# Products with C taken for two neighbouring tiles in one GpSimd instruction

## The chip, the core and the metric

The kernel runs on one core of a Trainium2 chip. The metric is device time in microseconds (us) of one execution, lower is better. Engines are called as in the profile: PE (matmul) with PEld (its weight loads), DVE (VectorE), ACT (ScalarE), POOL (GpSimd), SP (the queue that issues the DMAs).

## What is computed

Two layers of a selective state-space block (in-projection, 3x3 depthwise convolution, a scan in four directions, normalization, gate, out-projection) and two layers of attention without softmax and feed-forward in rounded formats, on 4 images of 64 x 64 tokens with 96 channels. Nearly all of the time goes to the scan of the first two layers:

```
def step(h, inp):
    u_t, dt_t, B_t, C_t = inp
    h = jnp.exp(dt_t[..., None] * A) * h + (dt_t * u_t)[..., None] * B_t[:, :, None, :]
    y = jnp.einsum('bkdn,bkn->bkd', h, C_t)
    return (h, y)
```

Here b is the image, k one of 4 directions, d one of 192 inner channels, n one of 16 states, and the scan runs over 4096 positions. For each (b, k, d, n) there is a row of decays exp(delta A), a row of inputs delta u B, the scan of the two, the product with C, and a sum over the 16 states n.

## The kernel before

**Tiles.** Two images are done together, so a layer is two phases, and there are four phases in all. A phase has K = 4 directions times 4 time blocks of TB = 1024 positions: 64 blocks. A block has 48 tiles of 128 x 1024, ordered by image i (2), group g of 32 channels (6) and quarter q of the states (4). The 128 partitions of a tile are 32 channels times 4 states. So there are 3072 tiles; I write tile n of a block as "place" n, 0 to 47, with place = 24 i + 4 g + q.

**One tile n** passes through these steps:

- *decays* (L781, ACT): exp(A delta), 128 x 1024, from `delta`, which `double` (L729) has read from DRAM with each channel repeated over 4 partitions.
- the input delta u B, in one of three ways. Ordinary tiles: PE spreads the B rows into PSUM (`row`, L766) and DVE multiplies them there by `du` (`product`, L788). *Turned* tiles (q = 3 but for g = 0): PE transposes ready products `bt` that ACT made (`fill`, L740). *Pooled* tiles (L37: q = 1, except image 1, group 3, which is place 37): POOL multiplies `du` by the repeated B row `brep` straight into the tile's buffer f (`ahead`, L760); the decays then go to PSUM.
- *scan* (L793, DVE): one scan instruction, from f and the PSUM tile psB into f.
- *remember* (L803, ACT): the last column is copied, as the start of the next block.
- *weigh* (L811, POOL): f is multiplied by the repeated C row `crep`, in place but one column to the left.
- *gather* (L837, PE): 4 matmuls sum over the 4 states of each channel, and over the four q, in a PSUM tile psY; `flush` (L855, ACT) and a DMA take it to `yd` in DRAM, from where `recall` and `resume` add it up over the directions.

**Order.** Every engine's queue is written out by hand in the loop at L1185. Step i of the loop issues work on several tiles: `double` for i+8, `recall` for i+5, `begin` (buffer and decays) for i+2, `ahead` for i+3, `remember` for i-1, `flush` for i-5, `gather` for i-3, `row` for i+2, `scan` of i, the decays of a pooled i+2, `product` of i+1, `weigh` of i. Each engine works its own queue in order and waits for semaphores. So POOL's queue has, in each group of four steps, four `weigh` and one `ahead`, and the `ahead` of tile n stands between the `weigh` of n-4 and of n-3.

**Beside it.** In each step the loop also issues a piece of background work: the convolution of a later phase or the end of an earlier one (L1248), and the preparation of the next block (`prepare`, L565): projections, softplus on ACT, three products `inputs` of 128 x 1024 on POOL (L651, L652), their stores to DRAM, and 48 transposes (`turn`, L663). In a block, `inputs` stand at places 30, 32 and 34, in the first direction of a phase at 34, 36 and 38.

**Buffers.** f has 8 buffers ("flow"), the repeated B and C rows share 8 ("rep"), delta and du together 6 ("dup"), psB and psY have 2 each. After the loop the feed-forward layers reuse these buffers (L1276): 15 tiles for tokens, 13 for transposed tokens.

Of the kernel before, what the change touches and what calls it, by code (L numbers as in the profile page):

```python
# [8 lines left out]
F32 = mybir.dt.float32  # L9
# [6 lines left out]
C = 96  # L16
D = 192
N = 16
# [3 lines left out]
L = HW * HW  # L22
T = 512
NT = L // T
TB = 1024
NTB = L // TB
J = 3
G = 6
Q4 = N // 4
# [5 lines left out]


def pooled(i, g, q):  # L37
    return q == 1 and (i, g) != (1, 3)


def turned(i, g, q):
# [4 lines left out]
def kernel(ctx: ExitStack, tc: tile.TileContext, ins, out, layers=(0, 1, 2, 3)):  # L46
    nc = tc.nc
# [7 lines left out]
    def st(shape, dtype, tag, bufs, name=None):  # L55
        return sp.tile(shape, dtype, tag=tag, name=name or tag, bufs=bufs)

    def psB():
        return ps.tile([128, TB], F32, tag="psB", name="psB", bufs=2)
# [5 lines left out]
        return ps.tile(shape, F32, tag="psM", name="psM", bufs=2)  # L65


    def rep(shape, name):
        return st(shape, F32, "rep", 8, name)

    def flow(shape, name, dtype=F32):
        return st(shape, dtype, "flow", 8, name)

    def part(shape, name):
        return st(shape, F32, "xt", 9, name)
# [2 lines left out]
    def wide(shape, name):  # L78
        return st(shape, F32, "wide", 4, name)
# [155 lines left out]
    def conv_pieces(w, xin, xc, zg, done, moments, settled):  # L235
# [1 line left out]
        norms = []  # L237

        def part_of(n):
            xb = st([C, T], F32, "dup", 6, "xb") if now[0] < 0 else wide([C, T], "xb")  # L240
            nc.sync.dma_start(xb, xin[n // NT][:, n % NT * T : (n % NT + 1) * T])
            return xb

# [3 lines left out]
        for i in range(2):  # L247
# [24 lines left out]
            t = small([C, 1], "grs")  # L272
# [439 lines left out]
    def rows_of(at, i):  # L712

        first = at * per + i * G * Q4
        out = []
        for q in range(Q4):
            for v in (0, 1):
                if v or any(pooled(i, g, q) for g in range(G)):
                    out.append((first + q - (7 if v else 9), at, i, v, q))
        return out  # L720

    def spread(task):

        _, at, i, v, q = task
        r = reps[at, i, v, q] = rep([128, TB], "crep" if v else "brep")
        row = 2 * N * v + N * i + 4 * q
        nc.sync.dma_start(r, made[at]["bc"][row : row + 4].unsqueeze(0).broadcast_to([32, 4, TB]))
# [12 lines left out]
    def fill(task):  # L740
# [4 lines left out]
        for h in range(4):  # L745
            nc.scalar.activation(  # L746
                b.rearrange("p (d h) -> p d h", h=4)[:, :, h], p["dut"][:, i, c, :], AF.Copy, scale=p["turns"][:, c, i, h : h + 1]
            )

    def begin(n):  # L750

        at, i, g, q = tiles[n]
        if pooled(i, g, q):
            scanned[n] = (psB(), early.pop(n))
            return
        f = flow([128, TB + 1], "f")
        scanned[n] = (psB(), f)
        decays(n, f[:, 1:])

    def ahead(n):  # L760

        at, i, g, q = tiles[n]
        f = early[n] = flow([128, TB + 1], "f")
        nc.gpsimd.tensor_mul(f[:, 1:], made[at]["dup"][1, i, g], reps[at, i, 0, q])  # L764

    def row(n):  # L766
        at, i, g, q = tiles[n]
# [35 lines left out]
    def remember(n):  # L803
        at, i, g, q = tiles[n]
        c = (i * G + g) * Q4 + q
        if blocks[at][2] < NTB - 1:
            if at not in states:
                states[at] = st([128, 2 * G * Q4], F32, "state", 2)
            nc.scalar.copy(states[at][:, c : c + 1], scanned[n][1][:, TB : TB + 1])  # L809

    def weigh(n):  # L811
        at, i, g, q = tiles[n]
        f = scanned[n][1]
        nc.gpsimd.tensor_mul(f[:, 0:TB], f[:, 1:], reps[at, i, 1, q])  # L814


    def recall(n):
# [19 lines left out]
    def gather(n):  # L837
        at, i, g, q = tiles[n]
        py = sums[at, i, g]
        f = scanned.pop(n)[1][:, 0:TB]  # L840
        for s in range(4):
            o = 3 - s if made[at]["back"] else s
            multiply(py[32 * o : 32 * o + 32, 0:U4], fold, made[at]["take"](f, s), start=False, stop=(q == Q4 - 1))
# [258 lines left out]

    def flushed(y):

        return L if y is not yd[-1] else max(0, (now[0] - 10) // per - (len(blocks) - NTB)) * TB

    def tail(ph, units=range(L // 256)):
        li, pair = phases[ph]
# [28 lines left out]
    made, reps, sums, states, scanned, early, order = {}, {}, {}, {}, {}, {}, [None]  # L1137
    end = len(tiles)
    now, rest = [-1], (L - TB) // 256
    with tc.manual_schedule(engines=MANUAL):  # L1140
# [41 lines left out]
        rows = sorted(row for at in range(len(blocks)) for i in range(2) for row in rows_of(at, i))  # L1182
        fills = [(at * per + i * per // 2 - 3 + c, at, i, c) for at in range(len(blocks)) for i in range(2) for c in range(NC)]
        waiting = []
        for i in range(-9, end + 6):  # L1185
            while rows and rows[0][0] <= i:
                spread(rows.pop(0))
            if 0 <= i + 8 < end and tiles[i + 8][3] == 0:
                double(i + 8)
            if 0 <= i + 5 < end and tiles[i + 5][3] == 0:  # L1190
                recall(i + 5)
            if 0 <= i + 2 < end:
                begin(i + 2)
            if 0 <= i + 3 < end and pooled(*tiles[i + 3][1:]):
                ahead(i + 3)
            while fills and fills[0][0] <= i:
                fill(fills.pop(0))
            if 0 <= i - 1 < end:
                remember(i - 1)
            if 0 <= i - 5 < end and tiles[i - 5][3] == Q4 - 1:  # L1200
                flush(i - 5)
            if 0 <= i - 3 < end:
                gather(i - 3)
                warm(i - 3)
            if 0 <= i + 2 < end:
                row(i + 2)
            if 0 <= i < end:
                scan(i)
            if 0 <= i + 2 < end and pooled(*tiles[i + 2][1:]):
                decays(i + 2, scanned[i + 2][0])  # L1210
            if 0 <= i + 1 < end:
                product(i + 1)
            if 0 <= i < end:
                weigh(i)
            at, place = divmod(i, per)
            now[0] = i
            if 0 <= i < end:
                if place == 4 and at % (K * NTB) == 0:
                    while aside is not None:
                        advance()  # L1220
                    aside = behind(blocks[at][0])
                plan = at + 1 < len(blocks)
                if plan:
                    if place == 0:
                        made[at + 1], nexts, kept = prepare(*blocks[at + 1])
                        for later, tasks in nexts.items():
                            todo[i + later] = todo.get(i + later, []) + tasks
                    ph1, k1, t1 = blocks[at + 1]
                    if place == min(nexts):
                        need = (t1 + 1) * TB // T if k1 == 0 else NT  # L1230
                        while done[ph1][0] < need:
                            advance()
                    if place == kept[0]:
                        while holds:
                            advance()
                    first = kept[-1] + 4
                    shut = done[0][0] == NT and (kept[0] - 3 <= place < kept[0] or first - 1 <= place < first + 6)
                for what, *arg in todo.pop(i, ()):
                    if what is made[at + 1]["turn"]:
                        waiting.append((what, *arg))  # L1240
                    else:
# [12 lines left out]
        now[0] = end + per  # L1254

        def remaining():
# [18 lines left out]
        spare = flow([128, TB], "spare")  # L1275
# [95 lines left out]
```

## Time and profile before

| what | value |
|---|---|
| time, median of 3 runs | 10528.52 us (10524.45 to 10543.51) |
| profiled execution, its own time | 10533.83 us |
| its span, first to last instruction | 10532.0 us |
| first and last scan start | 166.7 and 9912.1 us |
| POOL, products with C (L814) | 3072 x 2364 ns mean |
| POOL, inputs of pooled tiles (L764) | 704 x 2375 ns mean |
| POOL, `inputs` (L652) | 192 x 2367 ns mean |
| DVE, products with du (L791) | 1728 x 1210 ns mean |
| DVE, scans (L799) | 3072, 2271 to 2344 ns mean by form |
| ACT, copies of the last column (L809) | 2304, median 190 ns |

A duration runs from an instruction's start to its end; the records of two that follow each other overlap a little, so their spacing is what adds up. "Idle before" is the time that an engine stood still ahead of an instruction, and the name after the arrow is what it waited for last.

### The profile page before, as it was taken

How to read it: one execution, taken by the hardware profiler on the slowest of the kernel's cores; microseconds unless marked ns; L12 is line 12 of the kernel's file. 1: busy time of each engine (PE TensorE's matmuls, PEld its weight loads, DVE VectorE, ACT ScalarE, POOL GpSimd, SP SyncE). 2: the span in 40 equal slices, each digit the busy share in tenths (PEclk: the TensorE clock that was granted, in tenths of full speed). 3: DMA queues.
4: the chain of work that ended last, by engine and by line, in shares of the span. 5: the costliest groups of instructions: out<-in, count | busy, mean ns of one | idle time of the engine just before them, and what ended most of it. 6: DMA issues, size and time to landing. Idle time of an engine off the chain costs nothing. (4 is left out here: it accounts for less than half of the span.)

```text
span 10532.0 us, 158718 instructions
## 1 busy us (share of the span) xinstructions
PE 8643.6 (82%) x55291; PEld 4348.5 (41%) x55291; DVE 9423.1 (89%) x5975; ACT 8041.7 (76%) x16147; POOL 9645.1 (92%) x4848
## 2 busy tenths in 40 slices
PE   8998888777888887899878778898888787777777
PEld 2333333333444443333444444333444444334565
DVE  3889999999999999999999999999999999999746
ACT  4777787777788887878787877778777877677676
POOL 3899999999999999999999999999999999999756
PEclk8989898777878888989888888899878887878777
DMA  4568865686568865787555555555555555555310
GB/s 153 184 183 186 187 199 182 176 175 184 183 181 188 187 186 173 195 180 192 186 187 192 181 188 186 182 188 195 189 184 188 190 186 173 172 189 173 117 44 19
DMA packets 1993039, 1837.89 MB, mean 175 GB/s; under 512 B 1391850, under 2 KB 1610092, under 8 KB 1992236
## 3 DMA queue, kind: packets, MB, share of 16 engines
q1 hardware_dynamic: 1992236, 1827.73, 59.0%
q8 instruction: 437, 7.16, 0.3%
q14 instruction: 366, 3.00, 0.1%
HBM read 1439.38 MB, written 387.97 MB: 174 GB/s over the span
## 5 line engine op out<-in xcount | busy, mean ns | idle before, releaser
L814 POOL TENSOR_TENSOR f<-f,crep 128x1024 f32<-128x1024 f32 x3072 | 7186.3, 2364 | 421.9 <-DVE f L799 410.1
L799 DVE TENSOR_TENSOR_SCAN f<-f,state,psB 128x1024 f32<-128x1024 f32 x1776 | 4144.0, 2344 | 344.2 <-PE psB L137 181.2
L784 ACT ACTIVATE f<-delta,L_a 128x1024 f32<-128x1024 f32 x2368 | 2709.7, 1148 | 9.7 <-POOL f L814 1.8
L137 PE MATMUL psB<-spB,sel 96*128 96x512 bf16 x3456 | 1226.5, 442 | 1340.5 <-DVE f L799 1330.3
L791 DVE TENSOR_TENSOR psB<-psB,du 128x1024 f32<-128x1024 f32 x1728 | 2091.3, 1210 | 160.9 <-PE psB L137 156.3
L137 PE MATMUL psY<-f,fold 128*32 128x256 f32 x24576 | 2202.6, 442 | 7.7 <-POOL f L814 7.1
L137 PE MATMUL psB<-ident,bt 128*128 128x128 f32 x10240 | 1764.7, 343 | 215.8 <-DVE f L799 211.7
L137 PEld LDWEIGHTS psB<-ident,bt 128*128 128x128 f32 x10240 | 1627.7, 250 | 608.1 <-DVE f L799 373.3
L746 ACT ACTIVATE bt<-dut,bt 128x192 f32<-128x192 f32 x4096 | 1850.0, 614 | 34.6 <-PE psB L137 32.8
L764 POOL TENSOR_TENSOR f<-du,brep 128x1024 f32<-128x1024 f32 x704 | 1672.1, 2375 | 11.8 <-DMA du<-dud 10.3
L799 DVE TENSOR_TENSOR_SCAN f<-f,psB 128x1024 f32<-128x1024 f32 x592 | 1347.4, 2286 | 135.1 <-PE psB L137 68.3
L799 DVE TENSOR_TENSOR_SCAN f<-psB,state,f 128x1024 f32<-128x1024 f32 x528 | 1229.6, 2329 | 55.4 <-ACT psB L784 55.1
L784 ACT ACTIVATE psB<-delta,L_a 128x1024 f32<-128x1024 f32 x704 | 786.9, 1118 | 644.3 <-DVE f L799 643.2
L137 PEld LDWEIGHTS psY<-f,fold 128*32 128x32 f32 x24576 | 539.0, 115 | 1469.7 <-issue 931.5
L137 PEld LDWEIGHTS <-sel 96*128 96x128 bf16 x3456 | 210.2, 100 | 2216.4 <-DVE f L799 1813.2
L137 PE MATMUL psM<-pad,wf 96*64 96x512 f32 x3132 | 805.8, 624 | 7.5 <-ACT pad L309 5.8
L809 ACT COPY state<-f 128x1 f32<-128x1 f32 x2304 | 437.2, 193 | 268.2 <-DVE f L799 268.0
L671 ACT COPY dut<-psM 128x256 f32<-128x256 f32 x768 | 249.0, 377 | 471.6 <-PE psM L137 471.3
L652 POOL TENSOR_TENSOR xs<-delta,xs 128x1024 f32<-128x1024 f32 x192 | 454.3, 2367 | 63.2 <-ACT delta L649 63.2
L137 PE MATMUL psY<-yold,ident 128*128 128x256 f32 (+1 forms) x1344 | 466.7, 444 | 0.0
L137 PE MATMUL psM<-ident,xs 128*128 128x128 f32 x3072 | 438.0, 289 | 21.0 <-POOL xs L652 18.3
L137 PEld LDWEIGHTS psM<-ident,xs 128*128 128x128 f32 x3072 | 415.1, 202 | 84.0 <-POOL xs L652 28.0
(170 smaller groups left out, 8255.2 us busy)
## 6 DMA issues: line engine op xcount, KB each, us to landing
delta<-deltad SPq DMA_DIRECT2D x768, 512.0 KB
du<-dud SPq DMA_DIRECT2D x768, 512.0 KB
crep<-bc SPq DMA_DIRECT2D x512, 512.0 KB
deltad<-delta SPq DMA_DIRECT2D x192, 512.0 KB
dud<-xs SPq DMA_DIRECT2D x192, 512.0 KB
yd<-ynew SPq DMA_DIRECT2D x768, 128.0 KB
xraw<-xcd SPq DMA_DIRECT2D x144, 512.0 KB
yold<-yd SPq DMA_DIRECT2D x576, 128.0 KB
```

What stands on the lines that cost most here:

```text
L137: nc.tensor.matmul(out, lhsT, rhs, start=start, stop=stop, **kw)
L652: nc.gpsimd.tensor_mul(xs[j], deltas[j], xs[j])
L671: nc.scalar.copy(p["dut"][:, i, h * NC // 2 : (h + 1) * NC // 2, 64 * j : 64 * j + 64], m[:, :, 64 * i : 64 * i + 64])
L746: nc.scalar.activation(b.rearrange("p (d h) -> p d h", h=4)[:, :, h], p["dut"][:, i, c, :], AF.Copy, scale=p["turns"][:, c, i, h : h + 1])
L764: nc.gpsimd.tensor_mul(f[:, 1:], made[at]["dup"][1, i, g], reps[at, i, 0, q])
L784: nc.scalar.activation(out, made[at]["dup"][0, i, g], AF.Exp, scale=W[phases[ph][0]]["a"][:, k, g, q : q + 1])
L791: nc.vector.tensor_mul(scanned[n][0], scanned[n][0], made[at]["dup"][1, i, g])
L799: nc.vector.tensor_tensor_scan(f[:, 1:], a, bu, 0.0 if t == 0 else states[at - 1][:, c : c + 1], ALU.mult, ALU.add)
L809: nc.scalar.copy(states[at][:, c : c + 1], scanned[n][1][:, TB : TB + 1])
L814: nc.gpsimd.tensor_mul(f[:, 0:TB], f[:, 1:], reps[at, i, 1, q])
```

## The change

Two tiles 2p and 2p+1 (q = 0, 1 or q = 2, 3) now share one buffer f of 128 x 2 x 1025, and the C rows come in pairs too. `weigh` is issued at odd steps only, for both tiles: 1536 instructions on 128 x 2 x 1024 instead of 3072 on 128 x 1024. `remember` copies two columns at even steps. All q = 1 tiles are pooled, place 37 with them: 64 more `ahead` on POOL, 64 fewer `product` on DVE and 64 fewer pairs of `row` matmuls on PE. `gather` moves from i-3 to i-5, `flush` from i-5 to i-7, `resume` from i-2 to i-4. `double` moves from i+8 to i+6, with 4 buffers for delta and du instead of 6, `recall` from i+5 to i+3. f has 5 buffers of two tiles instead of 8 of one, C rows 3 buffers of two rows, the B row 2 buffers of its own. The tail has 13 tiles for tokens instead of 15, and 16 for transposed tokens.

```
 def pooled(i, g, q):
-    return q == 1 and (i, g) != (1, 3)
+    return q == 1
...
+    def flow():
+        return st([128, 2, TB + 1], F32, "flow", 5, "f")
...
     def rows_of(at, i):
         first = at * per + i * G * Q4
-        ...
-                    out.append((first + q - (7 if v else 9), at, i, v, q))
+        return [(first - 8, at, i, 0), (first - 6, at, i, 1), (first - 1, at, i, 2)]
     def spread(task):
...
+        _, at, i, v = task
+        row = 2 * N * (v > 0) + N * i + (4, 0, 8)[v]
+        if v == 0:
+            r = reps[at, i, "b"] = st([128, TB], F32, "brep", 2)
+            parts = [r]
+        else:
+            r = reps[at, i, v - 1] = st([128, 2, TB], F32, "crep", 3)
+            parts = [r[:, 0], r[:, 1]]
+        for m, to in enumerate(parts):
+            rows = made[at]["bc"][row + 4 * m : row + 4 * m + 4]
+            nc.sync.dma_start(to, rows.unsqueeze(0).broadcast_to([32, 4, TB]))
...
-            r = p["dup"][v, i, g] = st([128, TB], F32, "dup", 6, ("delta", "du")[v])
+            r = p["dup"][v, i, g] = st([128, TB], F32, "dup", 4, ("delta", "du")[v])
...
+    def place_of(n):
+        if n // 2 not in two:
+            two[n // 2] = flow()
+        return two[n // 2][:, n % 2]
     def begin(n):
+        scanned[n] = (psB(), place_of(n))
+        if not pooled(*tiles[n][1:]):
+            decays(n, scanned[n][1][:, 1:])
...
     def ahead(n):
         at, i, g, q = tiles[n]
-        f = early[n] = flow([128, TB + 1], "f")
-        nc.gpsimd.tensor_mul(f[:, 1:], made[at]["dup"][1, i, g], reps[at, i, 0, q])
+        nc.gpsimd.tensor_mul(place_of(n)[:, 1:], made[at]["dup"][1, i, g], reps[at, i, "b"])
...
-            nc.scalar.copy(states[at][:, c : c + 1], scanned[n][1][:, TB : TB + 1])
+            nc.scalar.copy(states[at][:, c : c + 2], two[n // 2][:, :, TB])
     def weigh(n):
         at, i, g, q = tiles[n]
-        f = scanned[n][1]
-        nc.gpsimd.tensor_mul(f[:, 0:TB], f[:, 1:], reps[at, i, 1, q])
+        f = two[n // 2]
+        nc.gpsimd.tensor_mul(f[:, :, 0:TB], f[:, :, 1:], reps[at, i, q // 2])
...
-        for i in range(-9, end + 6):
+        for i in range(-9, end + 8):
...
-            if 0 <= i + 8 < end and tiles[i + 8][3] == 0:
-                double(i + 8)
-            if 0 <= i + 5 < end and tiles[i + 5][3] == 0:
-                recall(i + 5)
+            if 0 <= i + 6 < end and tiles[i + 6][3] == 0:
+                double(i + 6)
+            if 0 <= i + 3 < end and tiles[i + 3][3] == 0:
+                recall(i + 3)
...
-            if 0 <= i - 1 < end:
-                remember(i - 1)
-            if 0 <= i - 5 < end and tiles[i - 5][3] == Q4 - 1:
-                flush(i - 5)
-            if 0 <= i - 3 < end:
-                gather(i - 3)
-                warm(i - 3)
+            if 0 <= i - 2 < end and i % 2 == 0:
+                remember(i - 2)
+            if 0 <= i - 7 < end and tiles[i - 7][3] == Q4 - 1:
+                flush(i - 7)
+            if 0 <= i - 5 < end:
+                gather(i - 5)
+                warm(i - 5)
...
-            if 0 <= i < end:
+            if 0 <= i < end and i % 2:
                 weigh(i)
...
-            if 0 <= i - 2 < end and tiles[i - 2][3] == 0:
-                resume(i - 2)
+            if 0 <= i - 4 < end and tiles[i - 4][3] == 0:
+                resume(i - 4)
...
-            "xt": several(6, [128, Q, C], F32, "dup", 6, "xt") + several(9, [128, Q, C], F32, "xt", 9, "xt"),
-            "tT": several(8, [C + 1, TB], F32, "rep", 8, "tT") + several(5, [C + 1, TB], F32, "flow", 8, "tT"),
+            "xt": several(4, [128, Q, C], F32, "dup", 4, "xt") + several(9, [128, Q, C], F32, "xt", 9, "xt"),
+            "tT": several(2, [C + 1, TB], F32, "brep", 2, "tT") + halves,
```

POOL's new queue in steps 4k-3 to 4k is: the pair (4k-4, 4k-3), `ahead` of tile 4k+1, the pair (4k-2, 4k-1). On PE, `gather` of tile n stands behind `row` of n+6 instead of n+4.

More of the change, by code (lines that the diff above doesn't have):

```diff
@@ L65, in psM @@
         return ps.tile(shape, F32, tag="psM", name="psM", bufs=2)
[L68 to L72, printed above, removed]
+    def flow():
+        return st([128, 2, TB + 1], F32, "flow", 5, "f")
     def part(shape, name):
@@ L239, in part_of @@
         def part_of(n):
-            xb = st([C, T], F32, "dup", 6, "xb") if now[0] < 0 else wide([C, T], "xb")
+            xb = st([C, T], F32, "dup", 4, "xb") if now[0] < 0 else wide([C, T], "xb")
             nc.sync.dma_start(xb, xin[n // NT][:, n % NT * T : (n % NT + 1) * T])
@@ L714, in rows_of @@
         first = at * per + i * G * Q4
[L715 to L718, printed above, removed]
-                    out.append((first + q - (7 if v else 9), at, i, v, q))
-        return out
-    def spread(task):
[L724 to L727, printed above, removed]
+        return [(first - 8, at, i, 0), (first - 6, at, i, 1), (first - 1, at, i, 2)]
+    def spread(task):
+        _, at, i, v = task
[9 more added lines that the diff above has]
+            nc.sync.dma_start(to, rows.unsqueeze(0).broadcast_to([32, 4, TB]))
     def double(n):
@@ L748, in fill @@
             )
+    def place_of(n):
+        if n // 2 not in two:
+            two[n // 2] = flow()
+        return two[n // 2][:, n % 2]
     def begin(n):
[L752 to L758, printed above, removed]
+        scanned[n] = (psB(), place_of(n))
+        if not pooled(*tiles[n][1:]):
+            decays(n, scanned[n][1][:, 1:])
     def ahead(n):
         at, i, g, q = tiles[n]
-        f = early[n] = flow([128, TB + 1], "f")
-        nc.gpsimd.tensor_mul(f[:, 1:], made[at]["dup"][1, i, g], reps[at, i, 0, q])
+        nc.gpsimd.tensor_mul(place_of(n)[:, 1:], made[at]["dup"][1, i, g], reps[at, i, "b"])
     def row(n):
@@ L840, in gather @@
         f = scanned.pop(n)[1][:, 0:TB]
+        if n % 2:
+            two.pop(n // 2)
         for s in range(4):
@@ L1103, in flushed @@
     def flushed(y):
-        return L if y is not yd[-1] else max(0, (now[0] - 10) // per - (len(blocks) - NTB)) * TB
+        return L if y is not yd[-1] else max(0, (now[0] - 12) // per - (len(blocks) - NTB)) * TB
     def tail(ph, units=range(L // 256)):
@@ L1136 @@
     per = 2 * G * Q4
-    made, reps, sums, states, scanned, early, order = {}, {}, {}, {}, {}, {}, [None]
+    made, reps, sums, states, scanned, two, order = {}, {}, {}, {}, {}, {}, [None]
     end = len(tiles)
@@ L1273, in several @@
             return [st(shape, dtype, tag, bufs, name) for _ in range(n)]
-        spare = flow([128, TB], "spare")
+        halves = [h for n, tag in ((3, "crep"), (4, "flow")) for t in several(n, [128, 2, TB], F32, tag, n + (n == 4), tag)
+                  for h in (t[0 : C + 1, 0], t[0 : C + 1, 1])]
+        spare = flow().rearrange("p m t -> p (m t)")
         pools = {
-            "xt": several(6, [128, Q, C], F32, "dup", 6, "xt") + several(9, [128, Q, C], F32, "xt", 9, "xt"),
-            "tT": several(8, [C + 1, TB], F32, "rep", 8, "tT") + several(5, [C + 1, TB], F32, "flow", 8, "tT"),
+            "xt": several(4, [128, Q, C], F32, "dup", 4, "xt") + several(9, [128, Q, C], F32, "xt", 9, "xt"),
+            "tT": several(2, [C + 1, TB], F32, "brep", 2, "tT") + halves,
             "tn": several(3, [128, Q, C + 1], F32, "delta", 3, "tn"),
```

## Prediction

> **What bounds the kernel now.** First the page's busy times, to see which engines can be the bound:
>
> ```profile
> PE 8643.6 (82%) x55291; PEld 4348.5 (41%) x55291; DVE 9423.1 (89%) x5975; ACT 8041.7 (76%) x16147; POOL 9645.1 (92%) x4848
> ```
>
> POOL and DVE are both near full. These shares hold a slow start (three blocks of about 170 us while the first convolutions run) and a tail of 620 us, so I read the table of stretches for the 61 blocks between:
>
> ```profile
> core 0: us, PE busy (x) PEld busy (x) DVE busy (x) ACT busy (x) POOL busy (x), PEclk, DMA share, GB/s
> 676.00:9912.00 9236.00, 7595.13 (x48668) 3728.91 (x48670) 8665.14 (x4804) 7184.68 (x14265) 8848.42 (x3893) 0.84 0.63 184
> ```
>
> There POOL is busy 95.8% and DVE 93.8%. Which one holds the other is told by the waits of the same stretch (total us, times, longest):
>
> ```profile
> PEld psY L137 <- POOL f L814: 332.2, 418, 1.6
> POOL f L814 <- DVE f L799: 324.2, 314, 4.2
> ...
> DVE f L799 <- PE psB L137: 238.7, 223, 5.7
> ```
>
> POOL's `weigh` waits for DVE's scan; DVE's scan waits for PE, never to speak of for POOL. So DVE with its PE stalls sets the pace, and POOL follows 0.1 to 5 us behind. But POOL has only 4% in hand, so I look at where in a block it is short. This is block 54, POOL alone, from place 28 on:
>
> ```profile
> 8481.58 4.66 POOL L814 TENSOR_TENSOR f<-f,crep 128x1024 f32<-128x1024 f32 x2 [1.22 <-DVE f L799]
> 8486.20 2.37 POOL L764 TENSOR_TENSOR f<-du,brep 128x1024 f32<-128x1024 f32 x1
> 8488.54 2.36 POOL L814 TENSOR_TENSOR f<-f,crep 128x1024 f32<-128x1024 f32 x1
> 8490.85 2.38 POOL L652 TENSOR_TENSOR xs<-delta,xs 128x1024 f32<-128x1024 f32 x1
> 8493.19 4.65 POOL L814 TENSOR_TENSOR f<-f,crep 128x1024 f32<-128x1024 f32 x2
> 8497.78 2.39 POOL L652 TENSOR_TENSOR xs<-delta,xs 128x1024 f32<-128x1024 f32 x1
> 8500.10 4.72 POOL L814 TENSOR_TENSOR f<-f,crep 128x1024 f32<-128x1024 f32 x2
> 8504.77 2.37 POOL L652 TENSOR_TENSOR xs<-delta,xs 128x1024 f32<-128x1024 f32 x1
> 8507.10 6.97 POOL L814 TENSOR_TENSOR f<-f,crep 128x1024 f32<-128x1024 f32 x3
> 8514.02 2.39 POOL L764 TENSOR_TENSOR f<-du,brep 128x1024 f32<-128x1024 f32 x1
> ```
>
> and DVE at its end:
>
> ```profile
> 8507.59 1.21 DVE L791 TENSOR_TENSOR psB<-psB,du 128x1024 f32<-128x1024 f32 x1
> ...
> 8520.56 2.33 DVE L799 TENSOR_TENSOR_SCAN f<-psB,state,f 128x1024 f32<-128x1024 f32 x1
> ```
>
> From 8481.58 on POOL never rests: the three `inputs` (L652) fall here, and place 37, in this very stretch, has no `ahead`. The L764 at 8514.02 makes the input of place 41 and ends at 8516.41; the scan that needs it starts at 8520.56. That slack, 4.15 us here, is on average 3.77 us over the 64 blocks (half of them 3.2 to 4.2, the least 1.1).
>
> **The change, part by part.**
>
> *Pairs on POOL.* In that timeline three `weigh` take from 8507.10 to 8514.02, four elsewhere 9.27 us: the spacing is 2.316 us, that of L764 2.33. What a pair saves is the part of an instruction that doesn't grow with its columns. Small instructions show it:
>
> ```profile
> 9994.08 0.21 POOL L925 TENSOR_TENSOR spare<-spare 128x8 f32<-128x8 f32 x1
> 9994.24 0.21 POOL L926 TENSOR_TENSOR spare<-spare 128x8 f32<-128x8 f32 x1
> ```
>
> 0.165 us apart for 8 columns. Then a column costs (2.316 - 0.165)/1016 = 2.117 ns, the fixed part is 0.148 us, and a pair takes 4.484 us. No instruction of two long rows is in the trace. The cheap bound is 4.40 (all of a small one's 0.21 us saved, and a little), the dear one 4.632 (two instructions' worth; a line through the 384 columns of L1045, 0.875 us apart, leaves next to no fixed part). I take 4.48, since L925 is the nearest in types: POOL does 1536 x 0.148 = 227 us less.
>
> *Place 37 pooled.* POOL gets 64 x 2.33 = 149 us, DVE loses 64 products of 1.21 us and their gap, 1.25 each in the spacing: **-80 us** on the engine that sets the pace. PE loses 64 pairs of `row` matmuls, behind other work: 0. Decays into psB can stall DVE: 81.1 us for 704 such tiles in the whole span, so **+7** for 64 more.
>
> *What is late next.* DVE's next wait is for POOL at place 41. Lay the new queue of block 54 against its recorded scans. Scan 29 ends at 8483.74. The pair (28, 29) can start only then, whereas the product of 28 was done before. From there to the end of `ahead`(41): 5 pairs, 3 `ahead` (33, 37, 41), 3 `inputs` of 2.34: 5 x 4.484 + 3 x 2.33 + 3 x 2.34 = 36.4 us, hence 8520.3 instead of 8516.4, 3.9 later. Scan 41 could start 1.25 earlier, at 8519.3. So DVE stalls 1.0 us there and keeps 0.25 of the 1.25. In general the stall is 3.9 + 1.25 - slack, with the mean slack 1.4 us per block. The same lay-out of POOL's queue over all 64 blocks, with the recorded ends of scans and DVE's stalls passed on, gives 81 us, 69 of them at place 41 and 12 at 45 (59 with pairs of 4.40, 102 of 4.55, 128 of 4.632). The same bookkeeping of the old queue gives POOL's recorded lag at every place to within 0.7 us. I take **+81**.
>
> The product with du takes 1210 ns on DVE (L791) and the one that replaces it 2375 on POOL (L764). The Trainium skill speaks against such a move: its page "GPSIMD Engine Reference", section "4.1 Engine selection", sends two-input elementwise work to VectorE, since GpSimd takes about twice as long; the two rows agree on the ratio. By that rule place 37 would have stayed on DVE, with neither the 80 us nor the 81, and the sum below would hardly differ.
>
> *Sums five behind.* A tile's sum needs both of its pair's products. Before, PE's `gather`(n) stood ahead of `row`(n+5), which needs scan n+3: with three steps of 9236/(61 x 48) = 3.15 us, 2.3 us for `weigh` and 0.6 for the matmuls, a lag of 6.6 us of POOL was free. Now the sum of a pair's first tile m stands ahead of `row`(m+7), which needs scan m+5, four steps after scan m+1: 12.6 - 4.5 - 0.6 = 7.5 us are free. In DVE's waits for psB, 69 us (66 cases) are ones where PE itself had waited for POOL after the PSUM tile was free. Between all of it kept and all gone I take half, **-35**; lags in the first half of a block get smaller by the lay-out, those at place 39 larger (5.1 us mean).
>
> *Pairs on ACT.* 1152 fewer copies of 190 ns, 219 us of ACT, which is busy 78% there. DVE waits 74 us for ACT in the main stretch: 0 to -20, I take **-5**.
>
> *Four delta and input buffers.* SP now waits in `double`(n) for product n-6 (before: n-10). From the end of that product to the first use, recorded: `ahead`(n+1) 12.9 us or more, decays (n) 7.6 or more, median 11.6. Laying the packets' bytes in the order of issues, these DMAs land 2.9 (delta) and 3.5 us (du) after issue, at most 7.9. Behind a waiting `double` on SP stand stores of `flush` and loads of `recall`, both with several steps in hand. Cost 0 to +10, taken 0. The second pair of C rows waits for the product of place 21 or 45 and has 11 us or more until its use; POOL already holds SP there 715 us without anyone waiting. Taken 0.
>
> *Later `inputs`.* Their third ends up to 2 us later, and `turn` on PE waits for it (28 us now): **+5** (0 to 20).
>
> *The end.* The last pair ends 2.2 us later, and two tiles fewer in the tail hold back two loads: **+5** (-10 to +20).
>
> Sum: -80 + 7 + 81 - 35 - 5 + 5 + 5 = **-22 us**. Against the profiled execution's 10533.83 us that is 10512; it lies 5.3 us above the median of the runs shown, so against the median I expect **10506 us**. A measurement of this kernel tells about 0.2% (21 us) from no change, so this is just on that bound.
>
> **The rivals.**
>
> *The stall at place 41 doesn't come* (15%). PE and ACT work on while DVE stalls, and the PE stalls after place 41 (30 us at place 43, 19 at 47, more in the next block's first places) could absorb it. For it: those stalls exist. Against: most of them are `row` work that starts only when a scan frees psB, so they move along with it. Then -80 + 7 - 35 - 5 + 5 + 5 = -103, **10425**; half absorbed, 10465.
>
> *The pair costs as much as two, so that the change doesn't do what it says and POOL becomes the bound in places 30 to 45* (33%). POOL then gets 149 us more and nothing back; the stall is 128 us, no PE wait goes: -80 + 7 + 128 + 5 + 5 - 5 = +60, **10588**, slower. It decides from about 4.55 us per pair on (102 us of stall, net zero). For it: the 384-column line. Against: the small rows.
>
> *A late delta* (7%). If one group in four gets its delta 1 us late, 192 us, 10700. Against: the leads above.
>
> *My forecast* (45%), 10480 to 10540.
>
> **The numbers.** Faster by over 0.2% (below 10507): half of my forecast's cases (0.24) and the first rival (0.15), 0.39. Within 0.2%: the rest of the forecast but its dear end (0.18) and the cheap end of the second rival (0.02), 0.20. Slower (above 10550): what is left of the second rival (0.31), the third (0.07) and the forecast's dear end (0.03), 0.41. The range goes from half-way into the first rival to the second's price: 10445 to 10590.
>
> **What would show it.** The group L814 with 128x2x1024: 1536 of some 4530 ns (duration; 4660 or more speaks for the second rival). A new row in the waits, DVE f <- POOL f L764, of 60 to 100 us, with place 41 in nearly all of it. DVE's L791 down by 64. PEld psY <- POOL well below 332 us. No row of ACT or POOL waiting for the DMAs of delta and du. I am wrong if DVE does not wait for POOL's L764 at all, or if it waits for POOL at places away from the `inputs`.

## The result and the profile after

The changed kernel takes **10670.28 us** (median of 4 runs, 10665.92 to 10674.65) against 10529.51 us before in the same runs: ratio 1.0132, 95% interval 1.0114 to 1.0149, 141 us slower. The forecast was 10506; the range ended at 10590. The profiled execution took 10665.92 us with a span of 10663.9.

The page's busy times of the changed kernel:

```profile
PE 8674.7 (81%) x55152; PEld 4351.0 (41%) x55152; DVE 9355.3 (88%) x5911; ACT 7949.7 (75%) x14995; POOL 9040.3 (85%) x3376
```

POOL has 605 us less to do than before and DVE 68 us less, and the kernel is slower. So neither is what was lost; a wait must have grown. The groups show the parts of the change at work (columns: count | busy us, mean ns of one | idle before it, its releaser):

```profile
L814 POOL TENSOR_TENSOR f<-f,crep 128x2048 f32<-128x2048 f32 x1536 | 6416.4, 4182 | 1142.1 <-DVE f L799 1103.2
...
L764 POOL TENSOR_TENSOR f<-du,brep 128x1024 f32<-128x1024 f32 x768 | 1813.5, 2361 | 23.3 <-DMA du<-dud 20.2
```

A pair lasts 4182 ns, and where nothing holds POOL up its next instruction starts 4.135 us after the pair (median of some 980 cases); I had taken 4.484, with 4.40 as the cheap bound. POOL is cheaper than forecast, and L764, the row that place 41 waits for, hardly holds up DVE. This is the whole span's wait of DVE for it, forecast at 60 to 100 us (us, times, longest):

```profile
DVE f L799 <- POOL f L764: 8.5, 12, 1.6
```

The waits between 676 and 10050 us, which cover the same blocks as before's 676 to 9912:

```profile
POOL f L814 <- DVE f L799: 985.6, 701, 4.9
...
DVE f L799 <- PE psB L134: 427.3, 279, 5.5
...
PEld psY L134 <- POOL f L814: 106.0, 160, 3.5
...
ACT f L784 <- DMA delta<-deltad: 63.2, 18, 8.4
```

POOL now waits for DVE three times as long as before (324.2), and PE waits for POOL a third as long (332.2), the latter as forecast. But **DVE waits for PE's psB 427 us instead of 239**. That wait I had expected to shrink.

To see which tiles it hits, I averaged for every place the time from the end of the scan before to the end of its own, over blocks 4 to 61, in both traces. Place 37 goes from 3.57 to 2.28 us, the product that left. Place 41 rises by 0.08. The intervals of the *turned* tiles (q = 3) rise: place 23 goes from 2.34 to 3.65, and 7, 11, 15, 31, 35, 39 and 47 rise by 0.17 to 0.34 each, all ten together by 3.4 us. A block takes 153.5 instead of 151.3 us. The first scan starts at 162.4 us and the last at 10038.9: the stretch between is 131 us longer, and the tail behind it 5 us.

Block 54 at place 23, before (start, us; the background work between left out):

```profile
8456.81 2.33 DVE L799 TENSOR_TENSOR_SCAN f<-psB,state,f 128x1024 f32<-128x1024 f32 x1
...
8458.77 0.64 PE L137 MATMUL psY<-f,fold 128*32 128x256 f32 x8
8459.05 1.21 DVE L791 TENSOR_TENSOR psB<-psB,du 128x1024 f32<-128x1024 f32 x1
...
8459.34 2.05 PE L137 MATMUL psB<-ident,bt 128*128 128x128 f32 x16
...
8460.36 4.59 DVE L799 TENSOR_TENSOR_SCAN f<-f,state,psB 128x1024 f32<-128x1024 f32 x2
```

Scan 21 frees its PSUM tile at 8459.1. `row`(23), the 16 transposes into it, starts 0.2 us later and ends at 8461.4, long before scan 22 does; scans 22 and 23 follow without a gap (one line, x2). The same place after:

```profile
8555.69 2.33 DVE L799 TENSOR_TENSOR_SCAN f<-psB,state,f 128x1024 f32<-128x1024 f32 x1
...
8557.93 1.21 DVE L791 TENSOR_TENSOR psB<-psB,du 128x1024 f32<-128x1024 f32 x1
...
8558.24 1.22 PE L134 MATMUL psY<-yold,ident 128*128 128x128 f32 x4
...
8559.24 2.35 DVE L799 TENSOR_TENSOR_SCAN f<-f,state,psB 128x1024 f32<-128x1024 f32 x1
...
8559.39 1.08 PE L134 MATMUL psY<-f,fold 128*32 128x256 f32 x8
8560.40 3.63 PE L134 MATMUL psB<-ident,bt 128*128 128x128 f32 x16
...
8564.15 2.35 DVE L799 TENSOR_TENSOR_SCAN f<-f,state,psB 128x1024 f32<-128x1024 f32 x1 [2.55 <-PE psB L134]
```

Scan 21 ends at 8558.0. PE now takes `resume` (psY<-yold) first, then `gather`, and only at 8560.40, 2.4 us after the tile was free, the transposes. They also last 3.63 us instead of 2.05. The granted clock (PEclk, the third column from the end) is 0.55 there and was 1.00 in the stretch of before, and 2.05/0.55 is 3.7:

```profile
8459.30:8461.40 2.10, 2.10 (x21) 1.94 (x18) 2.00 (x2) 2.04 (x6) 2.10 (x2) 1.00 0.35 127
...
8560.40:8564.10 3.70, 3.70 (x21) 3.58 (x18) 1.19 (x1) 2.16 (x8) 3.70 (x2) 0.55 0.58 171
```

DVE stands still for 2.55 us.

**The theory** from here on: `resume`(4k) stood at the end of step 4k+2, so that the next `row` on PE's queue was that of tile 4k+5, which is pooled and has none. Moved from i-2 to i-4 it stands at the end of step 4k+4, right ahead of `gather`(4k) and `row`(4k+7), a turned tile's 16 transposes, for which DVE has hardly any slack. **Rivals:** the pairs come too late for their sums; the four delta and input buffers; the later `flush`; the pooled place 37.

### The profile page after: what moved, and what is told of

Read it like the earlier page. It is cut to its first block, busy times and chain, and to the rows that moved or that the text cites. A ratio compares the mean times of both kernels' runs of the same rounds, so it can differ in the third digit from the quotient of the medians.

```text
span 10663.9 us, 154483 instructions
## 1 busy us (share of the span) xinstructions
PE 8674.7 (81%) x55152; PEld 4351.0 (41%) x55152; DVE 9355.3 (88%) x5911; ACT 7949.7 (75%) x14995; POOL 9040.3 (85%) x3376
## 5 line engine op out<-in xcount | busy, mean ns | idle before, releaser
L814 POOL TENSOR_TENSOR f<-f,crep 128x2048 f32<-128x2048 f32 x1536 | 6416.4, 4182 | 1142.1 <-DVE f L799 1103.2
L799 DVE TENSOR_TENSOR_SCAN f<-f,state,psB 128x1024 f32<-128x1024 f32 x1728 | 4035.2, 2345 | 482.3 <-PE psB L134 323.7
L784 ACT ACTIVATE f<-delta,L_a 128x1024 f32<-128x1024 f32 x2304 | 2613.3, 1144 | 106.1 <-DMA delta<-deltad 63.2
L791 DVE TENSOR_TENSOR psB<-psB,du 128x1024 f32<-128x1024 f32 x1664 | 2012.7, 1210 | 161.3 <-PE psB L134 152.0
L764 POOL TENSOR_TENSOR f<-du,brep 128x1024 f32<-128x1024 f32 x768 | 1813.5, 2361 | 23.3 <-DMA du<-dud 20.2
L134 PE MATMUL psB<-ident,bt 128*128 128x128 f32 x10240 | 1691.8, 332 | 15.6 <-DVE f L799 14.7
L784 ACT ACTIVATE psB<-delta,L_a 128x1024 f32<-128x1024 f32 x768 | 860.3, 1120 | 866.0 <-DVE f L799 861.9
L799 DVE TENSOR_TENSOR_SCAN f<-psB,state,f 128x1024 f32<-128x1024 f32 x576 | 1340.9, 2328 | 57.2 <-ACT psB L784 50.0
L134 PE MATMUL psY<-yold,ident 128*128 128x256 f32 (+1 forms) x1344 | 559.0, 523 | 0.0
L799 DVE TENSOR_TENSOR_SCAN f<-psB,f 128x1024 f32<-128x1024 f32 x192 | 435.7, 2269 | 26.2 <-ACT psB L784 24.4
```

The source lines that it names most:

```text
L134: nc.tensor.matmul(out, lhsT, rhs, start=start, stop=stop, **kw)
L764: nc.gpsimd.tensor_mul(place_of(n)[:, 1:], made[at]["dup"][1, i, g], reps[at, i, "b"])
L784: nc.scalar.activation(out, made[at]["dup"][0, i, g], AF.Exp, scale=W[phases[ph][0]]["a"][:, k, g, q : q + 1])
L791: nc.vector.tensor_mul(scanned[n][0], scanned[n][0], made[at]["dup"][1, i, g])
L799: nc.vector.tensor_tensor_scan(f[:, 1:], a, bu, 0.0 if t == 0 else states[at - 1][:, c : c + 1], ALU.mult, ALU.add)
L814: nc.gpsimd.tensor_mul(f[:, :, 0:TB], f[:, :, 1:], reps[at, i, q // 2])
```

## The experiments

Ratios are to the kernel before in the same runs, with 95% intervals. Differences in us are between medians; the kernel before itself came out at 10529.5 to 10534.8 in the five sets of runs, and the intervals reach 10 to 19 us to each side, so a difference between two runs is good to some 20 us. The waits shown are those between 676 and 10050 us. The number in a name such as "five behind" is `gather`'s distance.

**1. `resume` alone put back**, in the changed kernel.

```
-            if 0 <= i - 4 < end and tiles[i - 4][3] == 0:
-                resume(i - 4)
+            if 0 <= i - 2 < end and tiles[i - 2][3] == 0:
+                resume(i - 2)
```

> The changed kernel with one thing undone: `resume` is issued for tile i-2 again instead of i-4; `gather` stays five behind. Theory (order on PE): in the changed kernel `resume` (0.7 to 1.2 us of PE) falls into the step ahead of the turned tile's `row` (16 transposes, 2 to 3.6 us), where before it fell into the step ahead of a pooled tile, which has no `row`. Of the 3.4 us per block that scans of turned tiles gained, 2 to 2.5 go: 10520 to 10550 us; the wait of place 23 falls from 1.35 us to below 0.5. Rival A (four delta and input buffers, later transfers): 10670, unchanged. Rival B (sums wait for the coarser pairs): unchanged, 10670.

10598.77 us, 1.0063 (1.0048 to 1.0078): half of the loss goes, less than I expected. Place 23 is back at 2.35 us. A new wait takes the rest, for the PSUM tile that a `flush` seven steps behind frees too late:

```profile
PEld psY L134 <- ACT ynew L863: 563.6, 361, 6.2
...
PE psY L134 <- ACT ynew L863: 364.8, 255, 5.7
```

It hits places 18 and 19 (4.08 and 2.57 us instead of 3.57 and 2.35). So this run can't price `resume` by itself.

**2. All sums three behind**, as in the kernel before (`gather(i - 3)`, `flush(i - 5)`, `resume(i - 2)`), with the pairs.

> The changed kernel with the sums three behind as before: `gather` i-3, `flush` i-5, `resume` i-2; pairs, place 37, four buffers stay. Theory (order on PE): all 3.4 us per block of added waits at turned tiles go and the 80 us of place 37 stay: 10460 to 10500 us. Rival A (four buffers): 10670. Rival B (the pair's products come too late for the sums, so that five behind is needed): PE waits for POOL's L814 rise above 500 us and the time stays above 10600.

10748.69 us, 1.0204 (1.0189 to 1.0219): my expectation was wrong and the rival's right. Place 23 is back (2.39), but now PE waits for POOL's pairs, and DVE behind it at places 39 (5.21 us instead of 2.67) and 43 (3.44):

```profile
PEld psY L134 <- POOL f L814: 557.3, 422, 4.5
...
PE psY L134 <- POOL f L814: 341.4, 256, 4.3
```

**3. Sums four behind** (`gather(i - 4)`), with `flush` at i-6 and `resume` at i-3, in the changed kernel.

> The changed kernel with the sums four behind: `gather` i-4, `flush` i-6, `resume` i-3. Theory (order on PE): `resume` now falls into the step ahead of an ordinary `row` (0.6 us), so the 1.3 us of place 23 and most of the rest at turned tiles go; POOL's pairs leave a little less room than five behind, so places 39 and 43 (after POOL's `inputs`) may keep some of it: 10480 to 10540 us. If the sums themselves must be five behind for the pairs, 10600 or more, with place 39 as in the run with three behind.

10517.00 us, 0.9984 (0.9975 to 0.9993), as the theory said: 153 us under the changed kernel, with place 23 at 2.54.

**4. The order of the sums without the pairs**: the kernel before with `gather` at i-5, `flush` at i-7, `resume` at i-4, `double` at i+6, `recall` at i+3, four delta and input buffers, 9 buffers for f, and place 37 left on DVE.

> The kernel before, single tiles and place 37 on DVE, with the later sums (`gather` i-5, `flush` i-7, `resume` i-4, `recall` i+3), four delta and input buffers with `double` i+6, and 9 buffers f. Theory (order on PE): turned tiles wait as in the changed kernel, about 200 us more than before: 10690 to 10750 us. Rival B (pairs): 10530, as before. Rival A (four buffers) agrees with the theory here, and is told apart by the runs with the sums moved back.

10718.87 us, 1.0174 (1.0157 to 1.0191): the whole loss and more, without any pair and with place 37 on DVE. Place 23 is at 3.50. This clears the pairs and the pooled place 37.

**5. Only the four buffers**, in the kernel before (`double` at i+6).

> The kernel before with four delta and input buffers and `double` at i+6, nothing else. Theory: the leads of 7.6 us or more against landings of 7.9 at most cost nothing, 10525 to 10545 us, so that the 184 us of the kernel before with the later sums are those of the sums. Rival A: a good part of the 184 us, 10580 or more, with ACT waiting for the DMA of delta.

10563.54 us, 1.0023 (1.0013 to 1.0033): some 24 us (14 to 35) by the ratio, where I expected 10525 to 10545 us. Two waits are new:

```profile
POOL f L764 <- DMA du<-dud: 20.0, 11, 5.8
ACT f L784 <- DMA delta<-deltad: 19.7, 10, 4.7
```

They are few. Ahead of ACT's three longest (blocks 4 and 28) SP stands 4.6 to 6.1 us at a store of `flush` (L862), with `double` queued behind it. I had priced this at nothing. But the waits for the DMAs need not be what costs the 24 us: in this trace DVE's waits grow most at places 23 and 24, for PE (13.7 and 7.9 us), where none of the longer DMA waits falls. The way to the loss stays open.

**6. Only place 37 pooled**, in the kernel before, with single products.

> The kernel before with place 37 pooled and nothing else. The lay-out of the prediction for single tiles: `ahead` of place 41 ends 2.33 us later and its scan could start 1.25 earlier, against a mean slack of 3.77 us: DVE waits some 0.4 us per block there, so -80 + 7 + 25 = 10480 us. If POOL (92% busy) is the bound instead, 149 us of added POOL work shows: 10530 to 10600.

10591.41 us, 1.0055 (1.0040 to 1.0070), slower, where I expected faster. Place 37 falls to 2.28 as it should, but 39 rises by 1.19 us and 43 by 0.55:

```profile
PEld psM L137 <- POOL xs L652: 108.4, 47, 4.8
...
PE psM L137 <- POOL xs L652: 86.0, 44, 4.3
```

POOL's lateness doesn't reach DVE by way of L764; it goes through PE, which waits in `turn` for the third of the `inputs` with the next tile's `row` queued behind.

**7. The changed kernel with place 37 on DVE.**

```
-    return q == 1
+    return q == 1 and (i, g) != (1, 3)
```

> The changed kernel with place 37 back on DVE. With pairs of 4.14 us POOL has room, so place 37 should be worth its 80 us of DVE: 10740 to 10755 us. If it costs more than it gives, as it did with single tiles (57 us), 10600 to 10620.

10725.12 us, 1.0177 (1.0162 to 1.0192): 55 us slower than the changed kernel, a little less than the 70 to 85 that I expected. Pooling place 37 loses 57 us with single products (run 6) and gains 55 with pairs. The rule of the Trainium skill's page "GPSIMD Engine Reference", section "4.1 Engine selection", which the prediction weighed, says VectorE; here it would have cost those 55 us. That fits POOL's time in hand: it waits 986 us for DVE in the changed kernel.

**8. Five behind, with `flush` and `resume` a step earlier**, in the changed kernel.

```
-                flush(i - 7)
+                flush(i - 6)
...
-                resume(i - 4)
+                resume(i - 3)
```

> The changed kernel with `gather` five behind, but `resume` at i-3 and `flush` at i-6: `resume` falls ahead of an ordinary `row`, and the PSUM tile that it takes was flushed two steps earlier, as before. Theory (order on PE): 10460 to 10500 us, with neither the wait of place 23 nor PE's waits for ACT's `flush` that the run with `resume` at i-2 showed (928 us). If the place of `resume` is not the cause, 10600 to 10670.

**10498.57 us, 0.9963 (0.9948 to 0.9978)**: two lines, 172 us less than the changed kernel, faster than both. In the window (which here takes in 176 us of the tail) DVE's wait for psB is back where it was before the change:

```profile
DVE f L799 <- PE psB L134: 239.6, 238, 6.0
```

**9. `flush` alone a step earlier**, in the changed kernel.

> The changed kernel with `flush` one step earlier (i-6 instead of i-7) and nothing else. It is the other half of the best version, which moved `flush` and `resume` together. Theory (only the place of `resume` on PE's queue costs the time): 10650 to 10680 us, as the changed kernel, with the interval up to scan 23 still near 3.6 us. Rival (the late `flush` on ACT was what cost it): 10500 to 10550 us, place 23 near 2.4 us.

10679.03 us, 1.0143 (1.0126 to 1.0160), as the changed kernel; place 23 at 3.72. DVE's wait:

```profile
DVE f L799 <- PE psB L134: 398.4, 266, 6.1
```

Runs 8 and 9 differ in `resume` alone, by one step, so it is `resume`'s step that brings run 8's gain. That the `flush` has to come along is argued from run 1; `resume` at i-3 with `flush` at i-7 was not run.

**10. The order of run 8 without the pairs**: run 4 with `flush` at i-6 and `resume` at i-3.

> The kernel before, single products, place 37 on DVE, with the four delta and input buffers and sums five behind as in the changed one (9 buffers for f), but `flush` at i-6 and `resume` at i-3, so that `resume` doesn't stand ahead of a turned tile's `row`. Theory (sums five behind cost nothing by themselves, `resume`'s place cost some 150 us, the four buffers some 30): 10530 to 10580 us, against 10719 with `resume` at i-4; place 23 back to about 2.4 us. Rival (the later sums cost time with single products wherever `resume` stands): 10650 us or more.

10544.03 us, 1.0013 (1.0003 to 1.0023): 175 us less than run 4. With `resume` in this place, five behind costs nothing that shows beside run 5's buffers. What pairs and place 37 are worth together is the step from here to run 8: 1.0013 to 0.9963, 53 us.

The runs side by side. "Late" is the mean time from the end of scan 21 to the start of `row`(23) on PE, from the traces:

| kernel | `resume` | late, us | up to scan 23, us | block, us | time, us |
|---|---|---|---|---|---|
| before | i-2 | 0.43 | 2.34 | 151.3 | 10529.5 |
| changed | i-4 | 1.82 | 3.65 | 153.5 | 10670.3 |
| run 9 | i-4 | 1.93 | 3.72 | 153.6 | 10679.0 |
| run 4, single products | i-4 | 1.75 | 3.50 | 154.3 | 10718.9 |
| run 7, place 37 on DVE | i-4 | 1.86 | 3.72 | 154.5 | 10725.1 |
| run 8 | i-3 | 0.50 | 2.44 | 150.7 | 10498.6 |
| run 10, single products | i-3 | 0.40 | 2.34 | 151.3 | 10544.0 |

Whatever else differs, the four kernels with `resume` at i-4 are late and the others are not (runs 1 to 3 have 0.52, 0.44 and 0.60 us). It is so at all ten places of turned tiles: their `row` starts 0.67 us after its PSUM tile is free in the kernel before (mean of the ten places, blocks 4 to 61), 1.32 us in the changed one and 0.70 in run 8.

At place 23 the row is also slower: the 16 transposes last over 3 us in 5 of 58 blocks before, in 30 after and in 6 in run 8. Over all ten places, though, such slow rows become fewer, 246 of 580 before and 184 after, so a lower clock is not what all of them have in common. How much of place 23's 1.31 us is lateness and how much the clock was not told apart. Why the granted clock moves with the order was not tried.

**11. What a product of two rows costs on POOL, alone.** The first of three kernels of POOL products only.

> This kernel leaves all of the reference's computation out and writes zeros: it only issues products of two tensors on POOL, 8 of each form back to back: contiguous rows of 8 to 4096 columns, and the in-place product shifted by one column on 1x1024, 2x1024 and 2x512 columns, alone and beside scans on DVE. Theory (a column's price falls with the length of the instruction, and what was mis-sized in the prediction is the straight line through the short rows): 1x1024 spaced 2.29 to 2.33 us and 2x1024 4.10 to 4.17 us alone and beside scans alike, and the plain rows of 1024 and 2048 columns the same as the in-place ones, so the saving of about 0.5 us per pair belongs to the length, not to the shape. Rival (POOL is faster in the changed kernel only because something else on the chip leaves it more room): 2x1024 alone 4.45 to 4.63 us, twice the single one less a fixed part of 0.15 us or less.

Plain products of 2048 columns, the pair of the changed kernel, one such row of 1024, and two rows of 512 in one instruction (mean ns of 8):

```profile
L39 POOL TENSOR_TENSOR o<-a,b 128x2048 f32<-128x2048 f32 x8 | 35.7, 4493 | 0.0
...
L52 POOL TENSOR_TENSOR f<-f,c 128x2048 f32<-128x2048 f32 x8 | 33.2, 4156 | 0.0
...
L47 POOL TENSOR_TENSOR f<-f,c 128x1024 f32<-128x1024 f32 x8 | 18.5, 2337 | 14.6 <-DVE f L33 14.4
...
L57 POOL TENSOR_TENSOR f<-f,c 128x1024 f32<-128x1024 f32 x8 | 17.2, 2172 | 0.0
```

The straight line of the prediction was right for plain rows. The pair is cheaper, not for its length (two times 512 are cheaper than 1024 as well). Both theories named the length or the surroundings; both fall.

**12. Which part of the form saves**: two rows with a gap in some operands, in place or not, shifted by 1 or 8.

> This kernel leaves all of the reference's computation out and writes zeros: POOL products alone, 8 of each form: two rows of 1024 with a gap between rows in all, in some or in none of the operands, in place and not, two of 512, four of 256, 512 and 1024, one of 1024. Earlier, alone on the chip, the in-place 2x1024 took 4156 ns and the plain 2048 took 4493. Theory (rows with a gap in the operand that is written or read make a column cheaper, 1.94 instead of 2.10 ns): in-place 2x1024 4156 ns with gaps of 1 and of 16 columns alike, 4x512 the same, 4x1024 some 8130 against 8802 for 4096 plain ones, and rows without a gap, which the instruction can join into one, 4493. Rival 1 (the saving is a part per row, not per column): 4x256 is cheaper than the 2172 of 2x512 by as much as 2x512 is than 2338, 0.17 us. Rival 2 (being in place is what saves): 2x1024 with gaps that isn't in place takes 4493.

Of these forms, only those in place, shifted by one, with rows 1025 columns apart are cheap: 2x1024 4164 ns, 4x512 4223, 2x512 2219, 4x256 2229, 4x1024 8190. The same two rows not in place take 4518, and rows 1040 apart with a shift of 8 take 4508. The theory falls, and rival 1 with it. Rival 2's figure for rows not in place came about, but being in place is not enough: the rows 1040 apart and a single row (2402 ns) are in place too, and dear.

**13. On which column a row starts.**

> This kernel leaves all of the reference's computation out and writes zeros: POOL products alone, 8 of each form. Earlier forms told that only the in-place product shifted by one column whose rows start 1025 columns apart is cheap (4.16 instead of 4.50 us for 2x1024; 4.51 with rows 1040 apart and a shift of 8, and whenever it isn't in place). Theory (the second row is the cheap one, since it starts at an odd column: out on an odd column, in on the next even one): the second row of 1024 alone takes about 2.00 us, the first 2.34; rows 1040 apart that start on column 1 with a shift of 1 take 3.82 for two, those that start on column 0 4.50. Rival (what saves is the two rows in one instruction, wherever they start): each row alone takes 2.34 and two rows 1040 apart with a shift of 1 take 4.16 from column 0 and 1 alike.

First row and second row of a pair alone, then two rows 1040 apart, both begun on column 0 (L45) or on column 1 (L47):

```profile
L45 POOL TENSOR_TENSOR h<-h,c 128x2048 f32<-128x2048 f32 x8 | 35.6, 4483 | 0.0
...
L47 POOL TENSOR_TENSOR h<-h,c 128x2048 f32<-128x2048 f32 x8 | 30.2, 3807 | 0.0
...
L31 POOL TENSOR_TENSOR f<-f,c 128x1024 f32<-128x1024 f32 x8 | 18.4, 2336 | 6.9 <-DVE f L28 6.9
...
L33 POOL TENSOR_TENSOR f<-f,c 128x1024 f32<-128x1024 f32 x8 | 15.7, 1994 | 0.0
```

As the theory said: the saving is not in the pairing. The second row is cheap because of the column that it starts on. A row that writes from column 1, reads from column 2 and takes the other factor from column 0 costs 1.99 us; from 0, 1 and 0 it costs 2.34. Not in place it is 1.99 as well. A row written from column 1 and read from column 8 (2333 ns), or one whose other factor starts on column 1 (2336), is dear. Starting columns of the three operands that all differ modulo 4 fit every form of runs 11 to 13; why, no run tells.

**14. All rows of the cheap kind, in run 8's order.**

```
-        return st([128, 2, TB + 1], F32, "flow", 5, "f")
+        return st([128, 2, TB + 4], F32, "flow", 5, "f")[:, :, 1 : TB + 2]
```

> The best version so far (pairs, five behind, `flush` at i-6, `resume` at i-3) with each row of f begun one column later and rows 1028 instead of 1025 columns apart, so that both rows of a pair are of the cheap kind, not only the second. The pair should take 3.82 us instead of 4.17, POOL some 540 us less in all. Theory (POOL has time in hand in this version and DVE with its PE stalls is the bound): 10470 to 10500 us, little under 10499. Rival (the lag of POOL behind the scans still costs, by way of `gather` on PE: PE waits 145 us for it): 10400 to 10450 us.

**10471.91 us, 0.9940 (0.9923 to 0.9957)**, the fastest of all. A pair lasts 3815 ns, POOL has 550 us less to do, and the time falls by 27 us (the two intervals still overlap a little).

**15. The same in the kernel before**, single products.

> The kernel before, single products, with each f begun one column later (4 spare columns), so that every product with C is of the cheap kind: 2.00 instead of 2.34 us, 3072 x 0.34 = 1040 us of POOL in all, without any other change of the order. It asks what POOL's time was worth in the kernel before. Theory (DVE with its PE stalls sets the pace, POOL only follows; only the 69 us of DVE's waits behind PE waits for POOL can go): 10450 to 10520 us. Rival (POOL at 96% was a bound of its own): 10300 to 10400 us.

10527.38 us, 0.9993 (0.9984 to 1.0003), which is less gain than even the theory's 10450 to 10520 us. The page and the group:

```profile
PE 8687.3 (82%) x55291; PEld 4363.7 (41%) x55291; DVE 9411.9 (89%) x5975; ACT 8044.4 (76%) x16147; POOL 8585.9 (82%) x4848
...
L814 POOL TENSOR_TENSOR f<-f,crep 128x1024 f32<-128x1024 f32 x3072 | 6128.6, 2003 | 1456.1 <-DVE f L799 1418.3
```

POOL loses 1059 us of its 9645 and the kernel does not move. POOL, with the highest share of all engines, was worth nothing by itself here. Where POOL's time did pay was run 7, in which a product could be moved onto it (place 37).

## Why the prediction was wrong, step by step

**The step that failed is *Sums five behind*, "I take half, -35".** I counted how much of POOL's lag a later `gather` makes free. PE's wait for POOL did fall, from 332 to 106 us, but that is not this step's alone: with single products and a better place for `resume` (run 10) it falls from 353 to 310 us over the whole span. And the step moves `resume` too, and I didn't ask what stands behind it on PE's queue in its new place. It is the `row` of a turned tile. In place of -35 the order cost 172 us (changed kernel less run 8; 155 in single products, run 4 less run 5). With `resume` a step earlier the same five behind shows -11 us by the ratios and -20 by the medians, with an uncertainty of 15 (run 10 less run 5): at most a part of the gain of 35, and no loss from five behind as such. None of my rivals held it: all were about POOL or a DMA, none about the order on PE.

*Stall at place 41, +81:* 8.5 us in all. This was a size: 4.484 us for the pair, where it took 4.135, below my cheap bound of 4.40 too. Five pairs stand ahead of `ahead`(41), so that the error is 1.7 us per block, more than the mean slack that I found missing (1.4). The fixed part of 0.148 us was right for plain rows (run 11); half of the rows were of a cheaper kind, which none of the rows that I had read shows. Run 8, where DVE waits for PE no longer than before the change, keeps it at 11 us, so it isn't the new stalls that hide it.

*Place 37, -80:* place 37's interval falls by 1.29 us, 83 us in 64 blocks, as forecast; taking it back in the changed kernel costs 55 (run 7), good to some 20. With single products (run 6) the same edit loses, by a path that I had priced at +5 (`turn` waits for the `inputs`). *Later `inputs`, +5:* in the changed kernel PE waits 43 us for them, as before (25.5 and 17.1 us before, 26.3 and 16.4 after), nothing. *Decays into psB, +7:* DVE's wait for them went from 81.1 to 74.8 us, nothing. *Pairs on ACT, -5:* the copies take 217 us less, as counted, but ACT as a whole only 92; what of it reaches the end wasn't told apart. *Four delta and input buffers, 0:* 24 us (run 5), by a path that stays open. *The end, +5:* 617.6 to 622.6 us, as forecast, but this can't be told from scatter: runs 6 and 15, whose tail is that of before, have 613.7 and 622.4.

With the runs' values the sum is -83 + 0 + 9 + 172 + 24 + 5 = 127 us, against 141 measured. With run 7's 55 in place of 83 it is 155. Both are within what the single terms are uncertain by (some 20 us each).

Of my signs, the L764 wait (8.5 instead of 60 to 100) and the DMA waits (63 us for delta) told at once that DVE's loss lay elsewhere than forecast. The 128x2048 group at 4182 instead of 4530 ns spoke against my price and against the second rival alike.

## What to carry to other kernels

When a step of a queue written by hand is moved, write down for each instruction that moves what is queued behind it in the new place and how much slack that has. Here about a microsecond of PE work ahead of a turned tile's transposes cost up to 1.3 us a block at one place; a step earlier, ahead of an ordinary `row`, it cost nothing that shows. An engine's high share alone does not tell its worth: here 1059 us off the busiest engine gave nothing, and a move of two lines in the changed kernel gave 172. Price a new form of an instruction by itself before its count is multiplied by thousands.

## What the runs showed of the hardware

- A POOL product of 128 x 1024 in 32-bit takes 1.99 or 2.34 us depending only on the columns on which its operands start (run 13), and four spare columns took 15% off the products with C in the kernel before (2364 to 2003 ns, run 15).
- Beside scans whose two operands both lie in SBUF, POOL's products and DVE's scans take turns in run 11: single products follow each other every 4.28 us and pairs every 6.10, one scan to each, where a scan alone takes 2.18. In the kernel the scan reads one operand from PSUM, and neither is stretched in this way (4.135 us for a pair there, 4.11 alone; 2.27 to 2.35 us for a scan). The Trainium skill's page "SBUF — State Buffer", section "Who interferes with whom", says that a DVE instruction with two SBUF inputs contends with a GpSimd instruction that reads SBUF, and that one with at most one, outside the 2-port modes, does not; both cases agree.
- The same 16 transposes took 2.05 us at a granted clock of 1.00 and 3.63 at 0.55 in two traces of nearly the same work. At place 23 they last over 3 us in 5 of 58 blocks before, in 30 with the changed order of PE's queue, and in 12 in run 5, which leaves that order as it was.
